# Scanning inside sub-blocks with sixteen 32 by 32 products side by side, and a new order of the engines

## The chip, the cores and the metric

One core of one Trainium2 chip. The metric is the device time of one execution in microseconds (us). A program on one core is run several times, and I give the median and the range. A profile is one such execution; its span is 1.7 to 1.9 us shorter than the time of the same execution. Single executions of this kernel differ by up to 0.4%, so a difference of a few tenths of a us is read from ratios over several rounds, or not at all.

## The reference, cut to what matters

```python
h = relu(layernorm(x))                       # x is 4096 x 64
support = h @ weight
mask = (adj != 0)                            # adj is 4096 x 4096, f32: 64 MB
rank = cumsum(mask, axis=1); deg = rank[:, -1:]
k = minimum(deg, 100); pos = rank - (deg - k)
w = mask * where(pos > 0, 0.5 ** (k - pos), 0)
out = x + w @ support + bias
```

A neighbour's weight is a half to the power of the number of neighbours that come after it in its row. So the core of the kernel is a suffix count over each row of adj, an exponential, and a product with support.

## The kernel before: the parts that matter here

Adj comes in 64 pieces of 1 MB (128 rows by 2048 columns). Four pieces make a unit: 512 rows by half of the columns. For each piece VectorE (or ScalarE) converts to bytes, TensorE transposes, VectorE copies back. For each unit:

- `totals`: TensorE counts neighbours per sub-block of 32 columns; `split` (ScalarE) copies the counts to f16 ("sums"); `suffix` sums them over later sub-blocks; `clamp` (VectorE) writes `behind`.
- `place` puts the count behind each sub-block into a PSUM bank, and `scan` adds the count inside the sub-block:

```python
def suffix(u):                                # before
    ...
    if u % H:                                 # the other half of the row, done earlier
        nc.tensor.matmul(px, right, behind[u - 1], start=False, stop=True)

def place(u, a):                              # a bank for each block of 128 columns
    for c in range(CB):
        q = slice(SUB * c, SUB * (c + 1))
        v = vs[u, a * CB + c] = ps_v.tile([P, W], F32, tag="v", name="v")
        nc.tensor.matmul(v, where[q, a, :], behind[u][q, :], start=True, stop=False)

def scan(u, k):                               # a 128 by 128 product for each block
    nc.tensor.matmul(vs[u, k], tri, masks[u][:, k % CB, :, k // CB], start=False, stop=True)
```

- `weigh` (ScalarE) takes the exponential of a bank; `aggregate` (TensorE) multiplies it with `hr` and adds it up in one PSUM bank; `drain`, `turn_back` and `finish` end a group of two units.

A list scheduler in Python decides the order on every engine from a rank for each task. There are eight buffers for pieces and five `v` banks.

## Time and profile before

| | before |
|---|---|
| time, median of the runs beside the changed kernel (range) | 197.81 us (197.68 to 198.0) |
| span of the profile | 195.9 us |
| last piece of adj landed | 167.95 us |
| last `sums` start | 173.66 us |
| end of the last `weigh` | 189.2 us |

The landing comes from the trace's record of when each of the sixteen parts of a transfer has arrived; the other rows are from the timeline. The prediction below shows the page's main lines. Three more lines of the kernel before are needed later. First, the window from 35 to 160 us (length, then busy time and number of instructions of TensorE, its weight loads, VectorE, ScalarE and GpSimd, then the granted clock, the DMA share and GB/s):

```profile
35.00:160.00 125.00, 120.18 (x733) 72.56 (x732) 110.47 (x127) 116.12 (x117) 7.38 (x5) 1.00 1.01 420
```

Second, the page's line on the queue that brings instructions (packets, MB, share of the sixteen DMA engines), and third, from the view of the tile that adj lands in, the times from issue to landing of the pieces issued after 135 us:

```profile
q8 instruction: 8, 0.13, 0.3%
```

```profile
DMA to landing us min/median/max: 18.5/18.7/18.8
```

TensorE has 5 us to spare in this window. Late in the load, pieces land at an even 18.5 to 18.8 us after issue, as the others that are under way stand before them (18.7 us is 7.5 times the 2.49 us between two landings).

### The profile page before, as it was taken

The page shows a single profiled execution, that of the slowest core. Times are in us where ns is not written, and L with a number is a line of the kernel's source. Part 1 is how long each engine was busy: PE and PEld are TensorE (multiplying, and loading weights), DVE is VectorE, ACT ScalarE, POOL GpSimd, SP SyncE. Part 2 cuts the span into 40 slices and gives each one's busy share as a digit, 9 for nine tenths or more (in the row PEclk, how much of TensorE's full clock was granted, in tenths as well). Part 3 has the DMA queues.
Part 4 walks back from the last instruction along what each step waited for, and adds up shares of the span by engine and source line. Part 5 has one row for each costly group of instructions (what it writes and reads, how often), then busy time and mean ns, then how long its engine had stood idle before and what let it go on. Part 6 is the DMA issues. An engine that isn't in the chain of part 4 may idle for free.

```text
span 195.9 us, 2956 instructions
## 1 busy us (share of the span) xinstructions
PE 180.9 (92%) x1091; PEld 111.3 (57%) x1093; DVE 149.4 (76%) x210; ACT 167.0 (85%) x175; POOL 18.7 (10%) x30
## 2 busy tenths in 40 slices
PE   7699988999999996999999999999999999998981
PEld 2558934556665654656555646565645565645660
DVE  5862799999889876998898788987898789711102
ACT  2368769989898999599999999989998999899860
POOL 6000930000003000200030000300020001000100
PEclk9999999999999999999999999999999999999999
DMA  6999999999999999999999999999999999100000
GB/s 213 424 420 420 418 425 415 420 418 423 420 420 422 420 420 420 423 418 423 416 422 422 423 418 422 418 423 416 422 422 420 422 418 391 64 0 0 27 0 27
DMA packets 10381, 69.42 MB, mean 354 GB/s; under 512 B 1440, under 2 KB 1696, under 8 KB 2176
## 3 DMA queue, kind: packets, MB, share of 16 engines
q1 hardware_dynamic: 9728, 68.23, 84.1%
q0 software_dynamic: 336, 0.92, 1.3%
q8 instruction: 8, 0.13, 0.3%
q10 hardware_dynamic: 304, 0.10, 0.2%
q14 instruction: 5, 0.04, 0.1%
HBM read 68.19 MB, written 1.05 MB: 353 GB/s over the span
## 4 chain that ended last, share of the span: by engine, by line
DMA 61%; PE 22%; DVE 9%; POOL 3%; ACT 2%; issue 1%; SPq 1%; DVEq 0%; ACTq 0%
DMA a_sb<-in_adj_dram 61%; PE acc L372 9%; DVE m L308 6%; POOL rstd L271 3%; PE v L359 3%; PE pt L318 2%; PE pd L262 2%; PE pc L250 2%; ACT wk L364 1%; PE v L356 1%; PE po L391 1%; PE tot L333 1%; PE ps L344 1%; DVE xs L280 1%; DVE mt L327 1%
## 5 line engine op out<-in xcount | busy, mean ns | idle before, releaser
L364 ACT ACTIVATE wk<-v,floor 128x1024 fp32r<-128x1024 uint8 x128 | 133.4, 1133 | 10.3 <-PE v L359 10.2
L308 DVE TENSOR_SCALAR m<-a_sb 128x2048 uint8<-128x2048 f32 x62 | 86.0, 1392 | 16.3 <-DMA a_sb<-in_adj_dram 16.3
L372 PE MATMUL acc<-wk,hr 128*128 128x512 f32 x256 | 80.4, 432 | 0.4 <-DVE hr L290 0.4
L372 PEld LDWEIGHTS acc<-wk,hr 128*128 128x128 f32 x256 | 44.9, 188 | 18.7 <-issue 7.4
L318 PE MATMUL pt<-ident,m 128*128 128x128 f32 x256 | 44.5, 279 | 5.7 <-ACT sums L338 2.3
L327 DVE COPY mt<-pt 128x512 uint32<-128x512 uint32 x62 | 42.4, 685 | 2.5 <-PE pt L318 2.4
L318 PEld LDWEIGHTS pt<-ident,m 128*128 128x128 f32 x256 | 30.4, 141 | 24.5 <-issue 4.7
L359 PE MATMUL v<-mt,tri 128*128 128x512 f16 x128 | 42.3, 389 | 0.0
L400 POOL DMA_DIRECT2D out_dram<-o x7 | 9.1, 1296 | 147.6 <-DVE o L398 147.6
L338 ACT ACTIVATE sums<-tot 128x1024 f16<-128x1024 uint8 x16 | 16.5, 1034 | 2.3 <-PE tot L333 2.3
L359 PEld LDWEIGHTS <-tri 128*128 128x128 f16 x128 | 12.2, 97 | 7.0 <-issue 4.1
L350 DVE TENSOR_SCALAR behind<-ps,excess 128x512 f16<-128x512 f32 x16 | 12.0, 748 | 5.2 <-PE ps L346 5.2
L356 PE MATMUL v<-behind,where 32*128 32x512 f16 x128 | 12.6, 384 | 0.0
L333 PE MATMUL tot<-mt,band 128*32 128x512 f16 x128 | 10.1, 392 | 0.0
L344 PE MATMUL ps<-sums,later 128*128 128x512 f16 x32 | 9.5, 378 | 0.2 <-ACT sums L338 0.2
L356 PEld LDWEIGHTS <-where 32*128 32x128 f16 x128 | 3.3, 91 | 10.7 <-issue 10.7
L397 DVE TENSOR_TENSOR o<-po,xr 128x256 f32<-128x256 f32 (+1 forms) x9 | 3.5, 384 | 5.6 <-PE po L391 5.6
L271 POOL TENSOR_TENSOR rstd<-var,half 128x16 f32<-128x16 f32 x2 | 6.2, 3109 | 15.3 <-DVE var L267 15.3
L245 ACT ACTIVATE xt<-px 64x512 f32<-64x512 f32 x8 | 4.1, 586 | 4.0 <-PE px L241 3.9
L233 PE MATMUL none<-junk 128*128 128x512 bf16 x18 | 6.0, 474 | 1.4 <-DVE junk L126 1.2
L385 ACT ACTIVATE acc_sb<-acc,bias_sb 128x512 f32<-128x512 f32 (+1 forms) x8 | 5.5, 682 | 2.1 <-DVE acc_sb L383 1.7
L383 DVE TENSOR_SCALAR acc_sb<-acc,bias_sb 128x256 f32<-128x256 f32 x1 | 0.5, 485 | 8.4 <-PE acc L372 8.4
(75 smaller groups left out, 81.2 us busy)
## 6 DMA issues: line engine op xcount, KB each, us to landing
a_sb<-in_adj_dram SPq DMA_DIRECT2D x64, 1024.0 KB, 18.6
xr<-in_x_dram SPq DMA_DIRECT2D x2, 512.0 KB, 6.2
out_dram<-o POOLq DMA_DIRECT2D x7, 128.0 KB, 7.2
out_dram<-o ACTq DMA_DIRECT2D x1, 64.0 KB, 1.6
out_dram<-o SPq DMA_DIRECT2D x1, 64.0 KB, 1.7
w<-in_L_gnn_weight_dram ACTq DMA_DIRECT2D x2, 16.0 KB, 5.8
bias_sb<-in_L_gnn_bias_dram SPq DMA_DIRECT2D x1, 0.2 KB, 17.6
```

The lines of the kernel that those rows point to most:

```text
L271: nc.gpsimd.tensor_tensor(ns[i].rearrange("p b h -> p (b h)"), var.rearrange("p b h -> p (b h)"), half.to_broadcast([P, HB]), op=ALU.pow)
L308: nc.vector.tensor_scalar(m_v, a_v, 0.0, 64.0, op0=ALU.not_equal, op1=ALU.add)
L318: nc.tensor.transpose(pts[u, tt][:, c, :], m32[:, c * P:(c + 1) * P], ident)
L327: nc.vector.tensor_copy(mw, pt)
L333: nc.tensor.matmul(tot[SUB * c:SUB * (c + 1), :], band[:, SUB - 4 - 4 * a:2 * SUB - 4 - 4 * a], masks[u][:, c, :, a], start=(a == 0), stop ...
L338: nc.scalar.activation(sums8[u], pts.pop((u, "n")).bitcast(U8).rearrange("p (i f) -> p f i", f=4)[:, 1:3, :], AF.Copy)
L344: nc.tensor.matmul(px, later[:, f, :], sums[:, f, :], start=(f == 0), stop=(f == 1 and u % H == 0))
L350: nc.vector.tensor_scalar(behind[u], pts.pop((u, "s")), excess, float(MAX_NEIGH), op0=ALU.subtract, op1=ALU.min)
L356: nc.tensor.matmul(v, where[q, a, :], behind[u][q, :], start=True, stop=False)
L359: nc.tensor.matmul(vs[u, k], tri, masks[u][:, k % CB, :, k // CB], start=False, stop=True)
L364: nc.scalar.activation(wts[u, k], v, AF.Exp, scale=-LN2, bias=floor)
L372: nc.tensor.matmul(accs[0], hr[:, h * HB + k // CB * 2 * CB + s * CB + k % CB, :, :].rearrange("p s d -> p (s d)"), wk[:, s, :], start=((h ...
```

## The change

Intent: replace the four 128 by 128 scans of a group by sixteen 32 by 32 products that use the sixteen tiles of the array at once. For that, a bank holds one sub-block of four blocks, so that the four row tiles write different banks. Columns of adj and rows of x are taken in that order. The product with `right` becomes a copy of one row on GpSimd (`carry`), the two powers become Newton steps, four pieces are converted on ScalarE instead of two, and every rank is new.

```diff
+    def carry(u):
+        nc.gpsimd.tensor_copy(sums8[u][:1, 0, :], behind[u - 1][:1, :])
 ...
-        if u % H:
-            nc.tensor.matmul(px, right, behind[u - 1], start=False, stop=True)
 ...
     def place(u, a):
-        for c in range(CB):
-            q = slice(SUB * c, SUB * (c + 1))
-            v = vs[u, a * CB + c] = ps_v.tile([P, W], F32, tag="v", name="v")
-            nc.tensor.matmul(v, where[q, a, :], behind[u][q, :], start=True, stop=False)
-
-    def scan(u, k):
-        nc.tensor.matmul(vs[u, k], tri, masks[u][:, k % CB, :, k // CB], start=False, stop=True)
+        for j in range(4):
+            v = vs[u, 4 * a + j] = ps_v.tile([P, W], F32, tag="v", name="v")
+            q = slice(SUB * j, SUB * (j + 1))
+            nc.tensor.matmul(v, where[q, a, :], behind[u][q, :], start=True, stop=False, skip_group_check=True)
+        for c in range(4):
+            for j in range(4):
+                q = slice(SUB * j, SUB * (j + 1))
+                m = ...                       # cut: the mask of sub-block j of block c
+                nc.tensor.matmul(vs[u, 4 * a + j][SUB * c:SUB * (c + 1), :], tri[q, q], m, start=False, stop=True,
+                                 skip_group_check=True)
 ...
-        nc.gpsimd.tensor_tensor(ns[i]..., var..., half.to_broadcast([P, HB]), op=ALU.pow)    # two of these
+        nc.gpsimd.tensor_scalar(v, v, -0.5, None, op0=ALU.mult)
+        for i in range(3):
+            nc.gpsimd.tensor_tensor(t, y, y, op=ALU.mult)
+            nc.gpsimd.tensor_tensor(t, t, v, op=ALU.mult)
+            nc.gpsimd.tensor_scalar(t, t, 1.5, None, op0=ALU.add)
+            nc.gpsimd.tensor_tensor(y, y, t, op=ALU.mult)
 ...
-    signed = (4, 5)                           # pieces converted on ScalarE (cut)
+    signed = (2, 5, 6, 12)
+    shift, own = {...}, {...}                 # cut: a new rank for nearly every task
```

## The prediction

> **What bounds the kernel now.** I read the page's busy shares and slices first, then the chain of waits in order of time, then the groups by shape, who waited for whom on ScalarE, and the timeline of the last 40 us.
>
> ```profile
> PE 180.9 (92%) x1091; PEld 111.3 (57%) x1093; DVE 149.4 (76%) x210; ACT 167.0 (85%) x175; POOL 18.7 (10%) x30
> DMA  6999999999999999999999999999999999100000
> GB/s 213 424 420 420 418 425 415 420 418 423 420 420 422 420 420 420 423 418 423 416 422 422 423 418 422 418 423 416 422 422 420 422 418 391 64 0 0 27 0 27
> ```
>
> TensorE is the busiest engine, but the last two lines say more: the load of adj (64 pieces of 1 MB) runs at about 420 GB/s without a gap, from the first slice to slice 34 of 40. No change to compute makes that part shorter. The other 28 us are the tail.
>
> ```profile
> 131.84 18.73 DMA a_sb<-in_adj_dram
> ...
> 150.59 1.40 DVE m L308
> ...
> 185.67 4.59 PE acc L372 x20
> ...
> 190.36 0.50 DVE acc_sb L383
> ...
> 192.95 0.29 DVE o L398
> ```
>
> The chain agrees: up to 150 us it is load, one conversion, load, conversion; after that it is compute. It walks through TensorE, as TensorE never stands still there.
>
> ```profile
> L364 ACT ACTIVATE wk<-v,floor 128x1024 fp32r<-128x1024 uint8 x128 | 133.4, 1133 | 10.3 <-PE v L359 10.2
> L372 PE MATMUL acc<-wk,hr 128*128 128x512 f32 x256 | 80.4, 432 | 0.4 <-DVE hr L290 0.4
> L359 PE MATMUL v<-mt,tri 128*128 128x512 f16 x128 | 42.3, 389 | 0.0
> L356 PE MATMUL v<-behind,where 32*128 32x512 f16 x128 | 12.6, 384 | 0.0
> L271 POOL TENSOR_TENSOR rstd<-var,half 128x16 f32<-128x16 f32 x2 | 6.2, 3109 | 15.3 <-DVE var L267 15.3
> ```
>
> ```profile
> ACT wk L364 <- PE v L359: 9.7, 14, 2.1
> ```
>
> ScalarE is nearly full too: the exponentials (weigh, L364) are 128 of 1133 ns, and after 35 us it waits only 9.7 us for scans.
>
> ```profile
> 160.61 1.39 DVE L308 TENSOR_SCALAR m<-a_sb 128x2048 uint8<-128x2048 f32 x1 [0.53 <-DMA a_sb<-in_adj_dram]
> 168.04 1.39 DVE L308 TENSOR_SCALAR m<-a_sb 128x2048 uint8<-128x2048 f32 x1
> 172.31 0.64 PE L333 MATMUL tot<-mt,band 128*32 128x512 f16 x8
> 173.66 1.03 ACT L338 ACTIVATE sums<-tot 128x1024 f16<-128x1024 uint8 x1
> 174.56 5.16 ACT L364 ACTIVATE wk<-v,floor 128x1024 fp32r<-128x1024 uint8 x5
> 179.55 0.75 ACT L385 ACTIVATE acc_sb<-acc,bias_sb 128x512 f32<-128x512 f32 x1
> 180.12 4.20 ACT L364 ACTIVATE wk<-v,floor 128x1024 fp32r<-128x1024 uint8 x4
> 185.09 4.13 ACT L364 ACTIVATE wk<-v,floor 128x1024 fp32r<-128x1024 uint8 x4 [0.77 <-PE v L359]
> 185.31 4.94 PE L372 MATMUL acc<-wk,hr 128*128 128x512 f32 x20
> ```
>
> A piece landed just before 160.61 (the conversion waited for it). Pieces come every 2.49 us, so the last landed at about 168.0. The copy of the last unit's totals (sums, L338) starts 5.7 us later, then come 13 weighs, one drain and the aggregates. This tail is what can shrink.
>
> **What the Trainium skill says.** "TensorE: Matmul & The Clock Gate", Part 3, Packing small matmuls: products in different 32 by 32 tiles of the array run together, a pack taking one matmul plus about 4 ns per further tile; sixteen tiles measured 10.6 times faster. No run here shows sixteen yet. Four row tiles agree: L356's four of 384 ns take 0.40 us together (timeline at 174.02).
> "TensorEngine Tiling (Array Packing)", Key Properties: a change of tiling mode drains TensorE. The trace agrees: from the first of four L356 to the next 128-row product 0.32 us pass, where the stream is 0.215, so about 0.1 us for a switch. The same page, Gotcha 1, says that different row tiles need different PSUM banks. This is why one bank now holds one sub-block of four blocks.
> "ScalarE: Activation LUTs", What ACT_TABLE_LOAD costs: an ACTIVATE with a pointer bias takes 280 + 0.833 N ns and overlaps its successor by 93 ns. For 1024 that is 1133 ns, exactly the mean of L364. The measured step is (5.16 - 1.13)/4 = 1.01 us.
>
> **The change part by part.**
> Scan. Before, a group of four blocks costs TensorE a switch in (0.1), four row-tile places with the switch out (0.315), and four 128 by 128 scans of 0.22: about 1.3 us. After: 0.1 + 0.315, then sixteen products in one pass, 0.215 + 15 x 4 ns + about 0.1 for the second switch = 0.38. That is 0.8 us, 0.5 us less; over 32 groups 15 to 16 us of TensorE. The eight matmuls with `right` (0.215 each) leave as well, 1.7 us. In all about 17 us of 181 are freed, nearly all of it beside the load.
> Carry. Those eight matmuls become a one-partition copy on GpSimd between split and suffix in every odd unit; I put about 0.7 us on it (an estimate, from the 0.2 to 0.4 us that GpSimd's 128-column operations take here).
> Conversions. ScalarE takes four instead of two (2.53 us each). One more falls before the first weigh, one among the weighs.
> Root. Two powers (6.2 us) become three VectorE operations and 13 small GpSimd ones, about 2.6 us at an estimated 0.2 each. But in the new order of TensorE eight warm-up products stand between center and spread, and the third and fourth transposes come after spread. The first transpose stands among the turns of x and waits for the first conversion, so center starts about 1 us later than now (12.5). I get center done near 17, eight warm-ups to 18.7, spread (3.5 us as now) to 22.2, against 19.6 now. Then root 0.5, two copies of 0.7, totals, sums near 25.2, clamp near 29, the last two scales to 30.5, two hr copies: first weigh near 31.5 us, against 29.67. So the quick root buys nothing at the start.
> ScalarE's need. From first to last weigh: 128 x 1.01 + 15 x 0.9 (sums) + 7 x 0.57 (drains) + 2.4 + 0.5 = about 150 us; per unit 9.25 us, where four loads take 9.97. It starts some eight weighs behind and may catch up 0.7 us a unit. In the new order it does so: after the last sums stand 3 weighs, a drain and 8 weighs, where there were 5 and 8.
>
> The tail, followed along the new order of each engine with today's durations: VectorE does clamp 14 to about 166, conversion 62 to 167.4, two copies, and only then conversion 63: 169.0 to 170.4, although its data is there at 168.0. Transposes to 171.0, then place (14,1) stands ahead of the totals, so the ninth weigh before sums waits until 171.9. Sums start near 172.9 (173.66 before). Then 0.9 + 3 x 1.01 + 0.57: the first weigh of unit 15 at 177.5, suffix and clamp hidden under the three. Eight weighs with a short wait in the middle: last one done at 185.7 (189.2 before). Eleven pairs of aggregates follow the last place at 181.5, 22 x 0.232 + 0.2 = 5.3: done at 186.8 (190.26 before). The end (drain, turn back, add, store) is the same code and took 5.65 us: 192.4. Against a span of 195.9 this is 3.4 us less, so 194.3 us of time. If the stalls of ScalarE on the way exceed the 4 us that it has in hand (150 us of work from 31.5 end at 181.5, four before 185.7), the excess is added; I add 0.3 for that: 194.6.
>
> **The rivals.**
> (a) TensorE is the bound, and the time falls by its 17 us, to about 181. For it: 92% busy, the chain. Against it: the load lands at 168.0, and the last unit's own way (convert 1.4, transpose and copy 1.4, totals 0.6, split 1, suffix and clamp 1.4, place 0.8, eight weighs 8, aggregate 0.8, end 5.65) is 21 us, so nothing under 189 is possible even with a perfect order.
> (b) ScalarE becomes the bound and never catches up: later first weigh, one more conversion, waits for places because only five v banks serve groups of four. A place can finish only after the third weigh of the group before, and has about 0.9 us until the fourth is done. If each of some 30 groups costs 0.3 us, 9 us are lost where 4 are in hand: 199, no gain at all. For it: 9.7 us of such waits today, and the later start. Against it: today's waits are slack that the load's pace forces on ScalarE, and TensorE will be freer to answer.
> (c) The sixteen products do not overlap, by issue or by a semaphore each. At 60 ns a product the group is again 1.3 us and the time about 197; one after another at 0.215 it would be 3.4 us a group, 100 us in all, and far over 220. Against it: eight loads and matmuls of L333 start within 0.03 us in groups of four.
>
> **Range and chances.** The way along the tail gives 193.7 with no stall at all and each copy at its soonest, so over 2% faster (under 193.8) needs everything to go well or a tail shorter than I read it. Stalls of a few us more give 197. I take 194.6 us, with 192.8 to 197.2 for 8 in 10; faster 0.28, same 0.67, slower 0.05.
>
> **What would show it.** Right: DMA at 9 up to the same slice, last piece at 168; TensorE busy down by 10 to 20 us; the sixteen products of a group ending within 0.45 us; first weigh near 31.5; after 160 us sums starting at 172 to 174 and the last weigh ending at 185 to 187. Wrong: a first weigh before 29, a DMA that ends elsewhere, a last conversion at once on landing, waits of weigh for place over 6 us in sum after 35 us (rival b), or products that start over 20 ns apart (rival c).

## The result, and the profile after

The changed kernel is correct and took 195.38 us (median of 4 runs, 195.09 to 195.89) against 197.81 us beside it. The ratio is 0.9879, with a 95% interval of 0.9856 to 0.9902. Ratios here are the mean time of one kernel's fast runs over the mean of the other's fast runs of the same rounds, so not quite the ratio of the medians. All runs told here are of the fast state. The profiled execution took 195.28 us, with a span of 193.6 us.

First the page of the changed kernel: busy times, granted clock and DMA by slices, and the groups of the scan.

```profile
PE 170.6 (88%) x1479; PEld 103.9 (54%) x1479; DVE 147.9 (76%) x198; ACT 170.4 (88%) x177; POOL 23.0 (12%) x61
...
PEclk9999789999999999999999999999999999999999
DMA  6999999999999999999999999999999999500000
...
L405 ACT ACTIVATE wk<-v,floor 128x1024 fp32r<-128x1024 uint8 x128 | 133.0, 1143 | 3.9 <-PE v L400 3.8
```

TensorE has lost 10.3 us of busy time and is now no busier than ScalarE. After the last 9 the DMA row has a 5 where it had a 1. Part of this is only that the slices are shorter (4.84 us for 4.90), but 34 slices end at 164.6 us here, so the load runs well past that; the landings below give the time. `weigh` waits for scans for 3.8 us instead of 10.2. The window from 35 to 160 us says the same:

```profile
35.00:160.00 125.00, 112.97 (x1060) 66.18 (x1057) 111.03 (x127) 120.80 (x123) 12.20 (x12) 1.00 1.01 420
```

TensorE now has 12 us to spare there, and ScalarE does 4.7 us more of its work inside the window (123 instructions for 117). As its weighs begin later, little of this is left at 160 us: 28 of its instructions start after that, where it were 29. The timeline of the tail (start, duration):

```profile
164.77 9.49 ACT L405 ACTIVATE wk<-v,floor 128x1024 fp32r<-128x1024 uint8 x9
...
168.45 0.45 PE L400 MATMUL v<-mt,tri 32*32 32x512 f16 x16
...
170.13 1.40 DVE L339 TENSOR_SCALAR m<-a_sb 128x2048 uint8<-128x2048 f32 x1
...
174.17 1.01 ACT L373 ACTIVATE sums<-tot 128x1024 f16<-128x1024 uint8 x1
175.07 3.12 ACT L405 ACTIVATE wk<-v,floor 128x1024 fp32r<-128x1024 uint8 x3
178.06 0.71 ACT L430 ACTIVATE acc_sb<-acc,bias_sb 128x512 f32<-128x512 f32 x1
178.63 8.23 ACT L405 ACTIVATE wk<-v,floor 128x1024 fp32r<-128x1024 uint8 x8
```

All sixteen products of a group take 0.45 us together. After the last `sums` stand 11 `weigh` in place of 13, with one drain between and no gap, and the last ends at 186.86 us. The kernel before, at the same place in its timeline:

```profile
164.82 5.17 ACT L364 ACTIVATE wk<-v,floor 128x1024 fp32r<-128x1024 uint8 x5
170.65 3.13 ACT L364 ACTIVATE wk<-v,floor 128x1024 fp32r<-128x1024 uint8 x3 [0.67 <-PE v L359]
```

From 164.8 us on, the kernel before has 21 weighs left and waits twice for scans (0.67 us here, 0.77 us before its last four); the changed one has 20 left and doesn't wait. One weigh of 1.0 us and 1.44 us of waits make up the 2.4 us by which the last weigh ends sooner.

But the last conversion starts at 170.13 us, 2.1 us later than before, and the reason is the load. The piece before the last landed at 166.99 us (165.48 before) and was converted at once, at 167.09; in the new order two copies stand between that conversion and the last. The landings of the last piece, from the trace's records (time of the first of sixteen parts, then the lag of the last three behind it):

```
before   166.08   1.74  1.84  1.87     landed 167.95
after    166.03   1.86  3.23  3.42     landed 169.45
```

The first part is as early as before; two of the sixteen are 1.4 us later than the rest. This begins at one place. Up to 140.3 us every piece lands as before, within 0.2 us (one within 0.3); the next lands at 144.31, 1.5 us later than its like, and all after it are 1.5 to 2.0 us late. The view of adj's tile after 135 us, and the page's line on the instruction queue, of the changed kernel:

```profile
DMA to landing us min/median/max: 17.8/19.0/20.2
```

```profile
q8 instruction: 11, 0.18, 0.4%
```

TensorE's program has grown from 2184 to 2958 instructions, and that queue carries 11 packets of 16 KB instead of 8. The Trainium skill, "Advanced Engine Details and Errata", ISA Cache, gives a cache line of 16 KB for 256 instructions; 2958/256 is 11.6, and the trace's 0.18 MB in 11 packets agrees. "DMA: Bandwidth & Descriptors", Queues, rings and completion order, says that a DMA engine takes turns between its queues packet by packet. In the trace's records such a packet takes 1.02 to 1.33 us, and one starts at 142.0 us. The theory to test: **the changed scan pays part of its gain back through its own instruction stream, which delays adj.**

The chain of waits of the changed kernel (start, duration) shows that this delay matters. It leaves the load for the last time at that very piece:

```profile
124.04 20.27 DMA a_sb<-in_adj_dram
144.31 0.02 issue
144.34 1.39 DVE m L339
...
149.12 0.54 PE v L400 x14
149.66 0.02 ACT wk L405
...
154.74 1.71 POOL sums L376
...
182.58 5.34 PE acc L417 x22
```

From 144.31 us on the chain is compute alone, 49.3 us of it to the end of the span.

### The profile page after: what moved, and what is told of

It is laid out like the page before. It is cut to its first block, busy times and chain, and to the rows that moved or that the text cites. A ratio compares the mean times of both kernels' runs of the same rounds, so it can differ in the third digit from the quotient of the medians.

```text
span 193.6 us, 3765 instructions
## 1 busy us (share of the span) xinstructions
PE 170.6 (88%) x1479; PEld 103.9 (54%) x1479; DVE 147.9 (76%) x198; ACT 170.4 (88%) x177; POOL 23.0 (12%) x61
## 4 chain that ended last, share of the span: by engine, by line
DMA 38%; PE 27%; DVE 16%; ACT 11%; issue 4%; POOL 2%; DVEq 0%; POOLq 0%; ACTq 0%
DMA a_sb<-in_adj_dram 38%; DVE m L339 9%; PE acc L417 8%; ACT wk L405 7%; PE pt L350 5%; PE pp L302 2%; PE pc L263 2%; PE pd L279 2%; PE v L400 1%; DVE mt L361 1%; PE po L436 1%; ACT m L337 1%; DVE behind L388 1%; ACT sums L373 1%; PE px L254 1%
## 5 line engine op out<-in xcount | busy, mean ns | idle before, releaser
L339 DVE TENSOR_SCALAR m<-a_sb 128x2048 uint8<-128x2048 f32 x60 | 82.6, 1391 | 12.3 <-DMA a_sb<-in_adj_dram 11.6
L417 PE MATMUL acc<-wk,hr 128*128 128x512 f32 x256 | 75.7, 421 | 0.0
L350 PE MATMUL pt<-ident,m 128*128 128x128 f32 x256 | 42.5, 286 | 11.1 <-DVE m L339 6.5
L350 PEld LDWEIGHTS pt<-ident,m 128*128 128x128 f32 x256 | 28.0, 142 | 32.1 <-issue 11.6
L376 POOL COPY sums<-behind 1x512 f16<-1x512 f16 x8 | 6.0, 749 | 97.4 <-ACT sums L373 81.2
L400 PE MATMUL v<-mt,tri 32*32 32x512 f16 x512 | 14.3, 395 | 0.0
L337 ACT ACTIVATE m<-a_sb 128x2048 int8<-128x2048 f32 x4 | 10.1, 2514 | 1.6 <-DMA a_sb<-in_adj_dram 1.6
L367 PE MATMUL tot<-mt,band 128*32 128x512 f16 x128 | 10.3, 398 | 0.5
L246 PE MATMUL none<-junk 128*128 128x512 bf16 x30 | 9.4, 451 | 1.2 <-DVE junk L131 1.2
L400 PEld LDWEIGHTS <-tri 32*32 32x32 f16 x512 | 4.4, 88 | 9.9 <-issue 9.9
L436 PE MATMUL po<-ident,acc_sb 128*128 128x128 f32 x32 | 5.1, 281 | 2.3 <-ACT acc_sb L430 2.3
```

Source lines behind the costliest of these rows:

```text
L337: nc.scalar.activation(m_v.bitcast(I8), a_v, AF.Sign)
L339: nc.vector.tensor_scalar(m_v, a_v, 0.0, 64.0, op0=ALU.not_equal, op1=ALU.add)
L350: nc.tensor.transpose(pts[n][:, c, :], m32[:, c * P:(c + 1) * P], ident)
L367: nc.tensor.matmul(tot[SUB * c:SUB * (c + 1), :], band[:, SUB - 12 - 4 * a:2 * SUB - 12 - 4 * a], masks[u][:, c, :, a], start=(a == 0), st ...
L400: nc.tensor.matmul(vs[u, 4 * a + j][SUB * c:SUB * (c + 1), :], tri[q, q], m, start=False, stop=True, skip_group_check=True)
L417: nc.tensor.matmul(accs[g], hr[:, block(u, k) + 4 * s, :, :].rearrange("p s d -> p (s d)"), wk[:, s, :], start=(k == s == 0 and c0 + cb * ...
```

## The experiments

Two questions: what made the tail shorter (TensorE's time, the order, or both), and what made the load late. All diffs are against the changed kernel unless said otherwise. "Waits" is what `weigh` waits for scans after 35 us, from the view of who waited for whom (total, times, longest).

### Put TensorE's time back, keep the order

```diff
 def aggregate(u, k):
     ...
+    if k % 2 == 0:
+        nc.tensor.matmul(accs[g], junk[:, :P], junk, start=False, stop=False)   # adds zero
```

> The changed kernel, same order, with one more 128 by 128 product of zeros into the accumulator at every second aggregate: 64 x 0.215 = 13.8 us of TensorE work are put back, spread over the whole run, and no answer to a wait is made longer. My theory (the freed TensorE time lets ScalarE run nearly without waits): TensorE has 12 us idle between 35 and 160 us, the filler takes about 10 of them, the waits of weigh for place and scan after 35 us rise from 3.8 us to about 10, and the time is 197 to 199.5 us. Rival (the gain is the new order of the instructions and the four conversions on ScalarE, not TensorE's time): 195.4 within 0.5, waits as now.

```profile
PE 179.5 (92%) x1522; PEld 107.3 (55%) x1543; DVE 146.7 (75%) x198; ACT 170.9 (87%) x177; POOL 24.1 (12%) x61
```

```profile
ACT wk L405 <- PE v L400: 4.8, 11, 0.7
```

198.22 us (197.73 to 198.59, 12 runs), ratio to before 1.0025 (1.0015 to 1.0034). With TensorE back at 179.5 us the whole gain is gone, under an unchanged order. So the order alone doesn't carry it. The waits grew less than I thought, to 4.8 us. ScalarE's timeline shows where the loss arises:

```profile
164.61 4.16 ACT L405 ACTIVATE wk<-v,floor 128x1024 fp32r<-128x1024 uint8 x4
169.17 4.13 ACT L405 ACTIVATE wk<-v,floor 128x1024 fp32r<-128x1024 uint8 x4 [0.39 <-PE v L400]
173.92 1.11 ACT L405 ACTIVATE wk<-v,floor 128x1024 fp32r<-128x1024 uint8 x1 [0.62 <-PE v L400]
...
184.11 4.13 ACT L405 ACTIVATE wk<-v,floor 128x1024 fp32r<-128x1024 uint8 x4 [0.56 <-PE v L400]
```

At 164.61 us ScalarE is as far as the changed kernel at 164.77, with the same 20 weighs to do. It had been 1.1 us behind at 144 us (sums at 144.09 for 143.00), and made it up while both kernels waited for the late piece. So the products put back beside the load cost nothing that lasted, as that wait hid it; beside a load that isn't late up to 1.1 us might have shown. After 164.6 us three waits of 1.57 us in sum come in, and the last weigh ends 1.4 us later, at 188.24. Then the last 22 aggregates, with five added products among them, take 6.52 us instead of 5.40: another 1.1 us, paid directly. These two are the 2.5 us of span that are lost. The experiment shows that TensorE's time is dear in the tail; it does not show that its slack beside the load is worth anything.

### The same work where ScalarE waits for the answer

```diff
 def place(u, a):
         ...
+        if j == 3:
+            nc.tensor.matmul(v, junk[:, :P], junk, start=True, stop=True, skip_group_check=True)   # overwritten next
```

> The changed kernel, same order, with one more 128 by 128 product of zeros in each place, into the fourth bank and so between that bank's release and the sixteen products: 0.215 us and a change of tiling mode, about 0.4 us, 32 times, some 13 us of TensorE as in the run beside it, but all on the answer to ScalarE. A place can start its last product after the third weigh of the group before and has about 0.9 us; it needs 0.9 now. My theory (ScalarE paces from 45 us on and has nearly no slack): up to 0.4 us lost in each of some 30 groups, less what the load would have made it wait anyway: 200 to 207 us, more than the run beside it. Rival (only the sum of TensorE's time counts): the same as the run beside it. Rival (order alone): 195.4.

```profile
PE 185.4 (93%) x1509; PEld 110.2 (56%) x1511; DVE 147.4 (74%) x198; ACT 171.2 (86%) x177; POOL 23.1 (12%) x61
```

```profile
ACT wk L407 <- PE v L402: 8.5, 18, 1.0
```

200.27 us (200.0 to 201.96, 4 runs), ratio 1.0146. These 32 products stand between the third and the fourth place of a group, the 64 of the first experiment among the aggregates; half the number costs 2 us more. ScalarE does wait more, 8.5 us, and is 3.4 us behind at its drain near 160 us (163.66 for 160.31), where the first experiment was not behind at all. But TensorE is busy for 14.8 us more than in the changed kernel here, and for 8.9 us more in the first experiment, so the two runs differ in how much time was put back and not only in where. That the place alone makes the difference is not shown.

### The new operations in the old order

```diff
-    shift = {"aggregate": 56.5, ...}
-    own = {...}
+    shift, own = {}, {}          # with the old pieces on ScalarE and the old scheduler constants
```

> All new operations (sixteen products side by side, carry, Newton root, order of rows), but the instructions in the order that the ranks of the kernel before give them, and two conversions on ScalarE (pieces 4 and 5) as before. Thirteen weighs follow the last sums as in the kernel before, instead of eleven. My theory (the scan frees TensorE, but the tail gets shorter only because the new order lets ScalarE be two weighs further at the last sums): about 197 us, 196 to 198.5. Rival (the sixteen products give all of the gain, the order nothing): 195.4 within 0.5. Second rival (all from the order): 197.8 or over.

```profile
ACT wk L405 <- PE v L400: 6.2, 7, 3.1
```

```profile
178.87 13.29 ACT L405 ACTIVATE wk<-v,floor 128x1024 fp32r<-128x1024 uint8 x13
```

198.14 us (197.61 to 200.32, 19 runs), ratio 1.0029 (1.001 to 1.0048). The profiled execution was the longest of them (200.32), so its lines show shape, not size: 13 `weigh` stand after the last `sums` again. The new operations under these ranks gain nothing, and the first experiment showed that the new order gains nothing once TensorE's time is back. How much each is worth alone stays open: this is not the order of the kernel before (the first `weigh` of this profile starts at 39.16 us, there at 29.67), and the time contains the late load, which the pair of runs below puts at about 1.4 us. The late load is here too (last piece at 169.42 us, 11 packets), so it isn't the order that makes it late.

### Longer instruction stream in the kernel before: a failed test

This one edits the kernel before: after each store 110 short memsets on GpSimd, to bring more instruction packets.

> The kernel before with 110 small memsets on GpSimd after each of the first seven stores, 770 instructions more on an engine that has nothing else to do there. My theory of the late last piece (instructions are fetched in packets of 16 KB that hold one of the sixteen DMA engines for about 1 us; the load's pieces wait for the slowest engine, and an engine that is hit twice is 3.4 us behind where one hit once is 1.9): the instruction queue has about three packets more (11 instead of 8), and where two fall on one engine the last piece lands 1 to 1.5 us later and the time rises by as much, to 198.8 to 199.3; if all fall on different engines, no change. Rival (the late landing comes from when the kernel issues its loads or from chance, not from instructions): last conversion at 168.0 and 197.8 us, with more packets.

```profile
61.81 31.62 POOL L404 MEMSET pad<- 128x1 f32 x110
```

240.76 us (239.81 to 240.96), ratio 1.2166. A batch of 110 memsets took 31.6 us, 0.29 us from one to the next, so GpSimd issued its stores late and the whole kernel waited. As a test of time it says nothing. One thing it does show: GpSimd's packets came by another queue (q14, 11 instead of 5), while q8 stayed at 8, so q8's follow TensorE's program.

### Four of the sixteen products, then twelve tiny ones instead

Two runs that belong together. The first drops twelve of the sixteen products (a wrong result on purpose); TensorE's program falls to 2190 instructions, about as many as in the kernel before. The second puts the twelve back with one column each: 2958 instructions, but hardly any work (wrong on purpose too). The order on TensorE is unchanged in both.

```diff
 # scan1
-        for c in range(4):
+        for c in range(1):
 # scan1pad: range(4) again, and
+                i = slice(0, 1 if c else W)
-                nc.tensor.matmul(vs[...][SUB * c:SUB * (c + 1), :], tri[q, q], m, ...)
+                nc.tensor.matmul(vs[...][SUB * c:SUB * (c + 1), i], tri[q, q], m[:, i], ...)
```

> The changed kernel with one block's four of the sixteen products in each group instead of all sixteen (the result is wrong on purpose); the order on every engine is unchanged. TensorE's program shrinks from 2958 instructions to 2190, about what the kernel before has (2184). The theory on the late landing: the 16 KB packets of TensorE's instruction stream share the DMA engines with adj, and eleven of them instead of eight push one engine's parts 1.5 us back. Then this run has 8 or 9 such packets, its last piece lands at 168.0 us (plus or minus 0.3) with the sixteen parts spread over 1.9 us, and the time falls by 0.5 to 1.5 us to 194 to 195: the landing's 1.5, as far as ScalarE doesn't hold it, and not more, because sixteen side by side cost hardly more than four. Rival 1: the lateness comes from the new order or from chance; then the last piece lands at 169.4 as in the changed kernel. Rival 2: the products themselves cost time on the path (three quarters of them gone frees 32 x 0.2 = 6 us of TensorE): then the waits of weigh on scans fall well below 3.8 us and the time falls by more than 1.5 us.

> As scan1 (which ran in 194.0 us with 8 packets, last piece at 168.1), but the other twelve products of each group are put back as products of one column each (wrong result on purpose): TensorE's program has 2958 instructions again, as in the changed kernel, with little of its work. Theory: the number of instruction packets sets the landing: 11 packets, last piece at 169.2 to 169.8 us, the sixteen parts spread over 3.2 to 3.9 us, time 195.0 to 195.6. Rival: scan1 gained because three quarters of the products' time was gone: then the last piece lands at 168 as in scan1 and the time stays at 193.8 to 194.3.

With four products (page, view of adj's tile after 135 us, and chain of waits):

```profile
q8 instruction: 8, 0.13, 0.3%
```

```profile
DMA to landing us min/median/max: 17.8/18.6/18.7
```

```profile
124.15 18.80 DMA a_sb<-in_adj_dram
142.95 0.02 issue
142.97 1.42 DVE m L339
```

With the twelve tiny ones, the same three:

```profile
q8 instruction: 11, 0.18, 0.4%
```

```profile
DMA to landing us min/median/max: 17.8/19.3/20.3
```

```profile
124.67 20.29 DMA a_sb<-in_adj_dram
144.96 0.03 issue
144.99 1.38 DVE m L339
```

Four products: 194.01 us (193.65 to 194.19), ratio 0.9802 (0.979 to 0.9815), 1.4 us under the changed kernel. Tiny ones back: 195.35 us (195.03 to 195.86), ratio 0.9866 (0.985 to 0.9883), the changed kernel's time again. The piece that the chain hangs on takes 18.80 us with 8 packets and 20.29 us with 11. The last piece landed at 168.09 and at 170.10 us (this profile's load ran 0.3 us late from its start and 0.65 us from 114 us on, which puts the landing outside the 169.2 to 169.8 us that I expected), the sixteen parts spread over 1.83 and 3.39 us. From the landing of the piece that the chain hangs on to the end of the span are 49.3 us in the changed kernel, 192.0 - 142.95 = 49.1 with four products and 194.2 - 144.96 = 49.2 with the tiny ones. So the landing explains the whole difference.

This settles it: the lateness follows the number of instructions of TensorE, not their work and not the order. The other profiles agree: the last piece lands at 169.1 to 170.1 us in all ten with 11 or 12 packets, and at 168.0 and 168.1 us in the two with 8 (the failed test apart). It also falsifies the rival that the products' time costs: the work of twelve products of 512 columns in each group, 32 groups, can be taken out without gain once the instruction count stays. Side by side they cost little anyway: four take 0.41 us, sixteen 0.45. The waits did fall to 1.6 us with four products, but the 1.58 us wait that vanished is the one that the late piece had caused; with the tiny ones it is back (1.57 us).

The traces say which packet it is: the ninth. Its start, the landing of the first late piece, and the lag of the last part behind the first in the piece before that one and in that one:

```
              ninth packet   first late piece   lag before, then
fill             138.47          141.47           2.06    3.27
changed          142.01          144.31           1.88    3.41
oldranks         147.85          151.72           2.15    3.29
```

In each of the ten profiles with more than eight packets the lag rises by 1.1 to 1.7 us at the piece that lands 2.3 to 4.4 us after the ninth packet starts, and a second part falls behind after the tenth. With eight it stays near 1.9 us to the end. The first packet had done the same: in the kernel before, it starts at 21.88 us and the lag rises from 0.4 to 1.7 us at the piece that lands at 24.53 us (without warm-ups, where it starts at 23.94 us, at the piece that lands at 26.86 us). The seven after it put other parts back and hardly move the last one. So three packets more are not three equal costs; the landing moves with the first and with the ninth. That the ninth comes back to a DMA engine that had one already fits this, but is inferred: the trace doesn't name the engine of a packet. Nor does a run show why the lag of 1.5 us is longer than the 1.1 us of the packet.

### Small parts of the change, one at a time

```diff
 # nowarm: no eight warm-up products between center and spread
-            if f in (turn, spread, support, count, transpose, totals, suffix, place, aggregate):
+            if f in (turn, center, spread, support, count, transpose, totals, suffix, place, aggregate):
 # carryv: the carry on VectorE
-        nc.gpsimd.tensor_copy(sums8[u][:1, 0, :], behind[u - 1][:1, :])
+        nc.vector.tensor_copy(sums8[u][:1, 0, :], behind[u - 1][:1, :])
 # pow: the Newton steps out, two powers on GpSimd as before
```

> The changed kernel without the eight warm-up products between center and spread (1.9 us of TensorE at 16.5 us); everything else in the same order. Theory: they stand on the way to the first weigh, so that comes 1.3 to 1.9 us earlier (30.0 to 30.6 instead of 31.9), but the time falls by only 0 to 1.0 us (194.4 to 195.4): what limits the end is the landing of the last piece and ScalarE's work behind the sums, and an earlier start is worth only what ScalarE is still behind at 159 us. Rival: ScalarE is the bound from the first weigh to the last, and the time falls by the whole 1.5 us to 193.9. Third possibility: without the warm-ups the granted clock falls further than to 0.83 in the stretch from 20 to 30 us, and the time rises.

> The changed kernel with the carry copied by VectorE instead of GpSimd, the other engines' orders unchanged. Theory: the copy takes 0.25 us on VectorE instead of 0.60 (1.69 in one unit), and the 0.6 us wait of ScalarE at 159 us vanishes; VectorE has about 13 us free between 35 and 160 us, so its seven copies cost nothing. Time 0 to 0.6 us lower, 194.8 to 195.4. Rival: VectorE's order now holds the copy behind a conversion (1.4 us), and the suffix waits longer than for GpSimd: 0.3 to 1 us slower.

> The changed kernel with the two powers of the kernel before on GpSimd (3.1 us each) in place of the Newton steps (three operations of VectorE and thirteen of GpSimd that took 4.3 us). Theory: the root is not what the first weigh waits for, within about 2 us: first weigh 31.9 to 33.0 and time 195.2 to 196.2, that is 0 to 0.8 us slower; the root's part in the gain is nearly nothing. Rival: the root is on the path in full: then the first weigh moves by 1.9 us (6.2 minus 4.3) or more, and the time by over 1 us.

The first `weigh` of the changed kernel, of the one without warm-ups, and of the one with powers, in this order (timeline):

```profile
31.93 4.11 ACT L405 ACTIVATE wk<-v,floor 128x1024 fp32r<-128x1024 uint8 x4
```

```profile
29.85 4.11 ACT L405 ACTIVATE wk<-v,floor 128x1024 fp32r<-128x1024 uint8 x4
```

```profile
30.54 4.12 ACT L403 ACTIVATE wk<-v,floor 128x1024 fp32r<-128x1024 uint8 x4
```

| | time (range) | ratio to before | last piece landed | last `weigh` ends | between |
|---|---|---|---|---|---|
| changed kernel | 195.38 (195.09 to 195.89) | 0.9879 | 169.45 | 186.86 | 17.4 |
| without warm-ups | 195.19 (195.09 to 195.37) | 0.9865 | 169.62 | 186.66 | 17.0 |
| carry on VectorE | 195.60 (195.50 to 196.71) | 0.9893 | 169.81 | 186.83 | 17.0 |
| powers | 195.28 (195.13 to 195.42) | 0.9866 | 169.94 | 187.00 | 17.1 |

The intervals of these ratios overlap. Against the expectations: without warm-ups the first `weigh` came a little earlier than expected and the time fell by the small end of the range; the carry's small gain did not come; and with powers the first `weigh` came before the expected range, not in it. A start 2.1 us earlier is worth about 0.2 us (195.19 for 195.38), no more than the noise. That falsifies the rival that ScalarE is the bound from the first `weigh` to the last, which asked for 193.9 us. The quick root gains nothing: with powers the first `weigh` even came earlier, in an execution whose clock stayed at 1.00 between 20 and 30 us, where it was 0.83 in the changed kernel's. The carry costs 0.27 us on VectorE against 0.75 us on average on GpSimd, and moving it shows no gain either.

### The tail, and a try for a faster kernel

```diff
 # drainv: the drain of the last group but one on VectorE, which is idle there
-        if part == 1:
+        if part == 1 or g == G - 2:
 # best: drainv + nowarm + carryv, and the last sums on VectorE
+        if u == U - 1:
+            nc.vector.tensor_copy(sums8[u][:r], of)
```

> The changed kernel with the drain of the last group but one (0.57 us of ScalarE at 178.1 us) on VectorE, which is idle there; all else in the same order. Theory: from 159.3 us to the end of the last weigh ScalarE is the engine that sets the end, so the time falls by 0.4 to 0.6 us to 194.8 to 195.0. Rival: TensorE or the scans set the pace there; then weigh waits for a place as much as the drain took, and the time stays within 0.15 us of 195.38.

> A try for a faster kernel: the changed kernel without the eight warm-ups, with the carries on VectorE, and in the tail the last copy of totals (0.9 us) and the drain of the last group but one (0.57 us) on VectorE instead of ScalarE. If ScalarE sets the end of the tail, up to 1.5 us less, 193.9 us; but the scan of the last unit then becomes the next wait (sums on VectorE about 1.1 us, carry 0.3, suffix, clamp, place near 177.5 to 178), so that I expect 194.2 to 194.9. If the tail is bound by the landing and the way through the last unit's scan alone: 195.0 or more.

The drain alone: 195.47 us (195.02 to 195.71), ratio 0.9875 (0.9859 to 0.9891). No gain shows. In its profile the way from `sums` to the last `weigh` is 0.34 us shorter, but the last piece landed at 169.93, 0.48 us later than in the changed kernel's profile; an effect this small is lost among the landings, and the run decides nothing.

The combination: 194.73 us (194.63 to 194.85), ratio 0.9841 (0.9826 to 0.9855), the fastest correct kernel here, 1.6% under before and, by the ratios, 0.4% under the changed one. Its interval and the changed kernel's (from 0.9856) lie side by side without overlap, those of the kernels without warm-ups and with powers (from 0.9852) still touch it. Its timeline:

```profile
173.45 1.23 DVE L375 CAST sums<-tot 128x1024 f16<-128x1024 uint8 x1 [0.73 <-PE tot L367]
...
177.68 8.19 ACT L409 ACTIVATE wk<-v,floor 128x1024 fp32r<-128x1024 uint8 x8 [0.72 <-PE v L404]
```

`Sums` start 0.7 us earlier and ScalarE has 1.5 us less to do, but then waits 0.72 us for the last unit's scan, as expected: the tail is ScalarE's work and that scan's way, both nearly full. From the last landing to the last `weigh` are 16.4 us.

## Why the prediction was right or wrong

**The time** (194.6 us, range 192.8 to 197.2) was right: less than 2% faster, as was held most likely, inside the range, and 0.8 us low. The mechanism of the tail was right, and its sum nearly to the digit: from last landing to last `weigh` it said 185.7 - 168.0 = 17.7 us; measured 186.86 - 169.45 = 17.4 (before: 189.2 - 167.95 = 21.25). The steps between came as forecast, each 1.1 to 1.3 us late: last sums at 174.17 (172.9), first weigh of the last unit at 178.63 (177.5), last weigh done at 186.86 (185.7). The end part is 5.65 us as predicted.

**The term that was mis-sized** is the landing of the last piece: "last piece at 168". It was taken over from before as a thing that compute can't move. It landed at 169.45. The pair of runs with four and with twelve tiny products shows why: with 11 instruction packets instead of 8, the ninth and the tenth of which fall into the load, parts of adj are 1.5 us late. The tail got 21.25 - 17.41 = 3.84 us shorter and the load took 1.5 back: -2.34, against -2.3 in the spans and -2.4 in the medians. Without the late load the change would probably have been at the 2% line: the wrong-result run with 8 packets took 194.01 us, ratio 0.9802.

**The scan.** Sixteen products in one pass at 0.38 us: measured 0.45 us from the first start to the modelled end of the last, and 0.38 to the start of the next work (168.45 to 168.83). Right; rival (c) falls. That they cost little more than one row of four was shown by dropping twelve (0.41 us for four).

**TensorE's relief.** "About 17 us freed": the page has 10.3 us less. Counting each product in the two traces from its start to the start of the next on TensorE, places and scans take 25.2 us instead of 36.2: 0.79 us a group (forecast 0.8), but 1.13 before, where 1.3 was assumed, so 11.0 us are saved and not 15 to 16. The suffix with `right` falls from 8.4 to 4.3 us, and twelve more warm-up products, which the sum left out, take 3.2 us back. Rival (a), that the time falls by the relief, falls. That relief beside the load is worth little was right as far as the runs go: the first experiment put some of it back there without lasting loss. What counts is the relief in the tail, where `weigh` no longer waits (1.44 us) and one weigh fewer is left at 164.8 us.

**The start.** Spread to 22.2 and first `weigh` near 31.5: measured 21.83 and 31.93. Newton was put at 2.6 us; it took 4.3 (thirteen operations, 0.33 us from one start to the next). Neither shows in the end: without warm-ups or with powers, the time is the same within noise.

**Rival (b)**, ScalarE never catches up, was right in one thing: from 159.3 us to the last `weigh` ScalarE runs without a gap. It was wrong in the size of the waits, 3.8 us where the sign against me was over 6.

**The load's "9 up to the same slice"** looked right at a glance: the nines do end at the same slice, and slices of 4.9 us are too coarse for an error of 1.5. "A DMA that ends elsewhere" was among the signs named against the prediction.

## What to carry to other kernels

When a load runs without a gap, its end isn't a constant: what else moves over the same DMA engines, instructions of a longer program included, can move it. Count instructions before trading one product for four small ones, and test a suspicion like this by keeping the count and dropping the work. When you put an engine's time back to see what it is worth, read from the trace where the loss arises: here the products beside the load cost nothing that lasted, and those in the tail cost the whole 2.5 us of span.

## What the Trainium skill lacked or had wrong

- "Advanced Engine Details and Errata", ISA Cache, has the 16 KB line, and "DMA: Bandwidth & Descriptors", Queues, rings and completion order, the turns between queues, but neither says what it costs a load: here 3 packets more (11 instead of 8), each of 1.02 to 1.33 us, put the last of sixteen parts back by 1.5 us (spread 1.87 to 3.42 us), all of it from the ninth packet on, and the time by 1.3 us (194.01 to 195.35).
- "DMA: Bandwidth & Descriptors", Queues, rings and completion order, puts refills on row 14. In these profiles, if their queue numbers are the page's rows, the packets of kind "instruction" are on q8 (8 to 12, rising with TensorE's count) and on q14 (5 or 6, and 11 where GpSimd's program grew).
- "TensorE: Matmul & The Clock Gate", Part 3, Packing small matmuls: its table has 660 ns for a pack of sixteen, in a row that names no number of columns (the row for a pack of four has 512). Here a pack with 512 columns took 0.45 us at a granted clock of 1.00, and 0.38 us to the next product's start.
- No page that I read gives the cost of GpSimd's short operations: arithmetic on 128 by 32 f32 took 0.23 to 0.31 us, and 0.33 us from one start to the next, a copy of 1 by 512 f16 0.75 us on average (0.60 mostly, once 1.69; VectorE 0.27), a memset of one column 0.29 us from one to the next in long rows.
